# A two-layer image kernel (Fourier attention, then linear attention) on one core: its transfers merged into fewer and larger ones

## The chip, the core and the metric

The kernel runs on one core of one Trainium2 chip. Five engines work side by side: PE (TensorE, the matmuls), DVE (VectorE), ACT (ScalarE), POOL (GpSimd) and SP (SyncE, which here only issues transfers). Transfers are carried out by 16 DMA engines, which the core's issuing engines share; in this kernel nearly all are issued by SP, and those of the start by ACT as well. SBUF is the on-chip memory with 128 partitions, PSUM holds the matmuls' results, DRAM holds inputs, outputs and scratch.

The metric is the device time of one execution in microseconds. The kernel before has a median of 2763.84 us over three runs (2757.47 to 2765.46).

## What is computed

The input is a batch of 8 images of 256 channels and 96 x 96 pixels, f32. Cut to what matters, the reference is:

```python
def layer0(x, w1, b1, w2, b2, w3, b3, w_out, temperature):
    q, k, v = (fft2(conv1x1(x, w, b)) for w, b in ((w1, b1), (w2, b2), (w3, b3)))
    q, k, v = (t.reshape(b, 8, 32, 96 * 96) for t in (q, k, v))
    q, k = l2_normalize(q), l2_normalize(k)            # over the 9216 frequencies
    attn = einsum('bhcn,bhdn->bhcd', q, k) * temperature
    attn = complex(softmax(real(attn)), softmax(imag(attn)))
    out = abs(ifft2(einsum('bhcd,bhdn->bhcn', attn, v)))
    return conv1x1(out.reshape(b, 256, 96, 96), w_out)

def layer1(x, Wq, bq, Wk, bk, Wv, bv):                 # x as (b, 256, 9216)
    q, k = softplus(Wq x + bq), softplus(Wk x + bk)    # 32 channels each
    v = Wv x + bv
    return (q k-sum-normalised) @ (k v^T)              # linear attention

x = x + layer0(group_norm(x))
x = x + layer1(group_norm(x))
```

The group norm has 32 groups of 8 channels. The kernel doesn't take Fourier transforms of q, k and v. It gets the products of q and k out of sums over pixels, and replaces the transforms by a product of each image row with rows of its mirror image and by a fixed matrix R of 96 x 96 per row, which it calls rotating.

## The kernel before, in words

**Images and arenas.** The images are handled one after the other, image b+1's first part being woven into image b's last. Two large SBUF tiles (`arena`, 128 partitions x 2 halves x 9232 f32) take turns: image b's data is in `x_of(b)`, its rotated form in `y_of(b)`, which is the other arena. A half holds 128 of the 256 channels when the data is channel-major. In the first stage the arena's lower part (0 to `LO` = 4624) serves as staging space.

**Pair sums** (`pair_sums`, L342 to L415). The image's 96 rows are taken in pairs. A unit u (0 to 12) is four row pairs' worth on 128 partitions; two units are a double unit v = u // 2. `load_grouped` (L137) brings a double unit: f has the rows h and h+1 for four values of h, each on 32 partitions (4 DMAs of 192 KB), g has the mirror rows H-h and H-h-1, one at a time (8 DMAs of 96 KB). `turn_blocks(u)` (L355) copies the first element of every row of g behind its last (L361, once per double unit), transposes 32 x 32 blocks on DVE (L364, two instructions), and writes both turned blocks to a DRAM scratch `xtd` (L367, 2 DMAs of 384 KB). After an odd unit it issues the load of double unit v+2. The turned blocks have two places, by u % 2 (`turned_pair`). `pair(u)` forms their sum on POOL (L394) and their difference on DVE or POOL (L395; u = 0 and 12 on DVE alone, L390 to L392) into a tile `eo`, and sets its border columns (L385). `products` (L350) multiplies eo by itself on PE, 8 matmuls for each of three q; each q is a step of the generator. Around the products of unit u stand pair(u + 1), at q = 0, and turn_blocks(u + 2), at q = 1. The last unit (u = 12) is a single row.

**The tables** (`tables`, L249). Only once, beside image 0's pair sums: R's first form, computed on DVE, is written to DRAM (`rt`, L272), read back in 13 pieces in a skewed order (L279, `tm`), completed with two border columns and a tail by ACT (L290 to L292), and written out again as `rx` in 39 transfers (L295), one piece for each step of the generator. At the end comes `load_small` (L210): 55 small loads of biases and weights (L212 to L228), of which 32 are w_out's (`wo`). All are on ACT's queue. A POOL memset (L213) goes ahead of the biases `b12`.

**Rotating** (`rotate`, L595). `fetch` brings the turned rows from `xtd` back (L629, 192 KB: one direction c, two rows) and R's piece for four rows (L604) into one of 16 slots, which lie in the upper part of the image's arena; 14 steps ahead. `step` multiplies the rows by R on PE (L643) and copies the result into y (L649, L650). There are 49 steps an image, two for each even row h. From step 24 on, x itself is loaded again (`load_x`) in six pieces.

**The rest.** Layer 0's attention (`mix`), the image's complex parts (`images`, L666, with z on PE at L706, their magnitudes on DVE, POOL and ACT at L745 to L751, and w_out at L714), layer 1 (`layer1`, L765) and `output` (L939): there PE makes o (L974), DVE and POOL add it to x (L979, L983), and after both halves m of a piece s four DMAs (L995 to L997, 384 KB each) write the output, each with both halves.

**Order.** The order of the instructions on each engine is the order of the program text (a manual schedule); `weave` and the generators set what stands beside what. The main loop (L1011 on) runs image 0's pair sums with one step of `tables` at every index over 6, a `fetch` at every index over 20, and a `step` at every index over 26. In the later images the pair sums of b+1 are woven into `images(b)` and `layer1(b)`. Waits between engines and transfers are set by the framework from the memory that is touched; for an access that spans several rows of a tile it takes the whole stretch in between. [...]

## Time and profile before

| | |
|---|---|
| median of 3 runs | 2763.84 us (2757.47 to 2765.46) |
| profiled execution | 2761.41 us |
| its span | 2759.6 us |
| mean granted clock of TensorE | 0.959 |
| DMA packets | 388484, 413.37 MB, mean 150 GB/s |
| of these under 512 B | 144405 |
| SP's queue (q1) | 378880 packets, 406.20 MB, 53.5% of 16 engines |
| ACT's queue (q10) | 9400 packets, 4.49 MB, 0.7% |

The page's second section cuts the span into 40 equal slices of 69 us; a digit is the busy share in tenths. Its row for the DMA engines, and what they moved in GB/s:

```profile
DMA  7682736837185562746539274582736738177003
GB/s 173 189 259 50 182 81 199 246 58 186 53 272 172 120 164 73 237 147 148 136 106 290 72 177 107 163 259 56 184 79 222 223 69 197 36 240 221 1 7 138
```

The page's fifth section lists groups of instructions: line, engine, operation, out<-in, count, then busy time, mean ns of one, and idle time of the engine before them with what ended most of it. The page's sixth lists DMA issues by size. The groups that the change touches:

```profile
L350 PE MATMUL acc<-eo 128*128 128x257 f32 (+2 forms) x2368 | 439.7, 338 | 80.4 <-POOL eo L385 58.7
L394 POOL TENSOR_TENSOR eo<-arena 128x768 f32<-128x768 f32 x88 | 188.0, 2137 | 570.1 <-DVE ksum L901 254.4
L364 DVE STREAM_TRANSPOSE arena<-arena 128x768 f32<-128x768 f32 x192 | 175.8, 950 | 11.9 <-DMA xtd<-arena 8.9
```

In a list of waits, a line gives the waiting engine and line, what ended the wait, and then us in total, times, and the longest. A line of windows gives the stretch, its length, then busy us (and instructions) of PE, PE's weight loads, DVE, ACT and POOL, PE's granted clock, the DMA share and GB/s.

### The profile page before, as it was taken

To read this page: it belongs to the slowest core of one execution; us is meant where nothing else is said; L and a number is where in the kernel's file an instruction comes from. 1 tells how busy PE (TensorE), PEld (TensorE's weight loads), DVE (VectorE), ACT (ScalarE), POOL (GpSimd) and SP (SyncE) were. 2 spreads that over 40 slices of the span, in tenths; PEclk is the share of its full clock that TensorE was granted. 3 is DMA by queue.
4 is the path that set the end of the run, shared out by engine and by line. 5 is a ranking of instruction groups with operands and counts; after the bars stand their busy time and mean duration, and the time that the engine had idled before them with its cause. 6 is when DMAs were issued, how large, how long until landed. Compare 5 with 4: busy or idle time off the path is not lost. (4 is left out here: it accounts for less than half of the span.)

```text
span 2759.6 us, 41965 instructions
## 1 busy us (share of the span) xinstructions
PE 2553.8 (93%) x15580; PEld 1767.7 (64%) x15580; DVE 1804.9 (65%) x3441; ACT 1152.0 (42%) x1997; POOL 857.6 (31%) x801
## 2 busy tenths in 40 slices
PE   4499999999989999999999999999998999999987
PEld 3385666757667566766667566675666757667545
DVE  3257766577666767568675686657767577755766
ACT  0025353353534435344343544425353353524553
POOL 2203523135141451324412343213523135131311
PEclk8699999999999999899999999899999999989997
DMA  7682736837185562746539274582736738177003
GB/s 173 189 259 50 182 81 199 246 58 186 53 272 172 120 164 73 237 147 148 136 106 290 72 177 107 163 259 56 184 79 222 223 69 197 36 240 221 1 7 138
DMA packets 388484, 413.37 MB, mean 150 GB/s; under 512 B 144405, under 2 KB 339129, under 8 KB 388281
## 3 DMA queue, kind: packets, MB, share of 16 engines
q1 hardware_dynamic: 378880, 406.20, 53.5%
q10 hardware_dynamic: 9400, 4.49, 0.7%
q8 instruction: 124, 2.03, 0.3%
q14 instruction: 80, 0.65, 0.1%
HBM read 256.72 MB, written 153.86 MB: 149 GB/s over the span
## 5 line engine op out<-in xcount | busy, mean ns | idle before, releaser
L706 PE MATMUL z<-arena,mz 128*128 128x384 f32 (+1 forms) x2304 | 591.9, 488 | 0.0
L714 PE MATMUL po<-e,wo 128*128 128x384 f32 x1536 | 527.6, 487 | 1.7 <-ACT e L751 1.7
L750 POOL TENSOR_TENSOR e<-e 128x768 f32<-128x768 f32 x192 | 348.5, 1815 | 555.2 <-ACT e L749 528.5
L350 PE MATMUL acc<-eo 128*128 128x257 f32 (+2 forms) x2368 | 439.7, 338 | 80.4 <-POOL eo L385 58.7
L350 PEld LDWEIGHTS acc<-eo 128*128 128x128 f32 (+1 forms) x2368 | 386.5, 196 | 172.1 <-POOL eo L385 59.3
L706 PEld LDWEIGHTS z<-arena,mz 128*128 128x128 f32 (+1 forms) x2304 | 310.2, 163 | 234.6 <-issue 50.5
L643 PE MATMUL y<-tm,arena 96*128 96x128 f32 x3072 | 407.3, 289 | 31.5 <-ACT ys L650 12.6
L643 PEld LDWEIGHTS y<-tm,arena 96*128 96x128 f32 x3072 | 382.9, 201 | 77.3 <-issue 26.3
L714 PEld LDWEIGHTS po<-e,wo 128*128 128x128 f32 x1536 | 290.0, 190 | 204.7 <-ACT e L751 7.3
L745 DVE TENSOR_TENSOR e<-z,xT 128x768 f32<-128x768 f32 x384 | 361.8, 950 | 85.2 <-PE z L706 85.0
L749 ACT ACTIVATE e<-e 128x1536 f32<-128x1536 f32 x192 | 284.5, 1482 | 195.6 <-DVE e L745 194.0
L394 POOL TENSOR_TENSOR eo<-arena 128x768 f32<-128x768 f32 x88 | 188.0, 2137 | 570.1 <-DVE ksum L901 254.4
L716 DVE TENSOR_TENSOR arena<-arena,po 128x384 f32<-128x384 f32 x384 | 209.8, 552 | 192.9 <-PE po L714 192.9
L751 ACT ACTIVATE e<-e 128x768 f32<-128x768 f32 x192 | 162.0, 844 | 366.0 <-POOL e L750 362.1
L983 POOL TENSOR_TENSOR arena<-arena,po 128x384 f32<-128x384 f32 x180 | 179.3, 1015 | 292.5 <-ACT po L982 292.3
L306 DVE BATCH_NORM_STATS2 st<-arena 128x6 f32<-128x384 f32 x384 | 194.3, 548 | 0.0
L364 DVE STREAM_TRANSPOSE arena<-arena 128x768 f32<-128x768 f32 x192 | 175.8, 950 | 11.9 <-DMA xtd<-arena 8.9
L650 ACT COPY ys<-y 128x4 f32<-128x4 f32 (+1 forms) x200 | 32.6, 163 | 348.3 <-DVE arena L649 304.1
L875 PE MATMUL xT<-ident,arena 128*128 128x128 f32 x1152 | 157.9, 291 | 3.0 <-ACT xT L878 3.0
L982 ACT COPY po<-o 128x384 f32<-128x384 f32 x180 | 78.4, 485 | 183.5 <-PE o L974 178.9
L875 PEld LDWEIGHTS xT<-ident,arena 128*128 128x128 f32 x1152 | 138.7, 150 | 23.2 <-issue 13.6
L649 DVE COPY arena<-y 128x384 f32<-128x384 f32 (+1 forms) x200 | 108.8, 544 | 67.6 <-PE y L643 52.9
(225 smaller groups left out, 2512.8 us busy)
## 6 DMA issues: line engine op xcount, KB each, us to landing
xtd<-arena SPq DMA_DIRECT2D x192, 384.0 KB
arena<-xtd SPq DMA_DIRECT2D x384, 192.0 KB
arena<-in_x_dram SPq DMA_DIRECT2D x96, 768.0 KB
out_dram<-arena SPq DMA_DIRECT2D x192, 384.0 KB
arena<-in_x_dram SPq DMA_DIRECT2D x192, 192.0 KB
arena<-in_x_dram SPq DMA_DIRECT2D x384, 96.0 KB
tm<-rx SPq DMA_DIRECT2D x96, 159.0 KB
wl<-in_w1t_dram SPq DMA_DIRECT2D x8, 256.0 KB
```

The costliest lines, as they stand in the source:

```text
L306: nc.vector.bn_stats(out=st[:, k, c, :], in_=x_of(b)[:, k, c * CH:(c + 1) * CH])
L350: nc.tensor.matmul(acc[c][:, m * (C + 1):m * (C + 1) + C + 1 - m * P], lhsT=eo[0:np_, q, c, 1 + m * P:1 + (m + 1) * P], rhs=eo[0:np_, q, c ...
L394: nc.gpsimd.tensor_add(e, ft, gt)
L643: nc.tensor.matmul(pu[:, o:o + P], lhsT=xt[:, s, k * P:(k + 1) * P], rhs=tm[:, n:n + P], start=True, stop=True)
L706: nc.tensor.matmul(out[:, 0:CH].rearrange("p (h q) -> p h q", q=PR), lhsT=columns(mz, k, c, j), rhs=yz[:, k, f, :, o:o + PR], start=(k == ...
L714: nc.tensor.matmul(po[:, 0:CH], lhsT=wo[:, k, m * P:(m + 1) * P], rhs=e[:, k, :], start=(k == 0), stop=(k == KC - 1))
L716: nc.vector.tensor_add(x[:, m, n], x[:, m, n], po[:, 0:CH])
L745: nc.vector.tensor_add(e[:, 2 * c:2 * c + 2, :].rearrange("p t (q h) -> p t q h", h=H), pz[:, 0:CH].rearrange("p (h q) -> p q h", h=H).uns ...
L749: nc.scalar.activation(e, e, AF.Square)
L750: nc.gpsimd.tensor_add(e[:, 0:2, :], e[:, 0:2, :], e[:, 2:4, :])
L875: nc.tensor.transpose(pt[:, j * C + k * P:j * C + (k + 1) * P], x[:, k, o:o + P], ident)
L983: nc.gpsimd.tensor_add(x[:, m, r], x[:, m, r], t)
```

## The change

R is read back in one piece and written out in four transfers; it is completed by three ACT instructions in place of 39, in a part of the second arena that is free at the start. The table helpers on DVE move behind R. `load_small` has 28 transfers instead of 55 (w_out's first half, the temperatures and the layer-1 biases in one transfer each or nearly so) and yields between batches, so it goes on from step to step; `tables` is started before the loop and goes on from index 4 instead of 7. The mirror rows of g are loaded in pairs, in their order in memory (4 DMAs instead of 8; at h = 0 they stay single), and the transpose reads them backwards. The copy behind the rows' ends becomes two copies through a small tile `wrap`. The turned blocks of a double unit lie together, in one place per direction; one DMA of 1.5 MB, issued after the odd unit, writes them all, where four of 384 KB were. A `fetch` brings both directions of a row pair (384 KB), into 7 slots; it is called half as often. `output` issues the write of a half m right after its adds, two DMAs for each m.

```diff
     def turned(b):
-        o = NB8 * 2 * (2 * W + 1)
-        return [x_of(b)[:, u % 2, o + i * NQ * C:o + (i + 1) * NQ * C] for i in range(2)]
+        return [x_of(b)[:, c, TO:TO + 2 * NQ * C].rearrange("p (q r n) -> p q r n", q=NQ, r=2) for c in range(2)]
...
-            nc.sync.dma_start(out=f[s].rearrange("p c r w -> p c (r w)"), in_=xs[:, :, h:h + 2].rearrange("p c r w -> p c (r w)"))
-            for r in range(2):
-                nc.sync.dma_start(out=g[s, :, r, 0:W], in_=xs[:, :, (H - h - r) % H])
+            nc.sync.dma_start(out=f[s], in_=xs[:, :, h:h + 2].rearrange("p c r w -> p c (r w)"))
+            if h:
+                nc.sync.dma_start(out=g[s], in_=xs[:, :, H - h - 1:H - h + 1].rearrange("p c r w -> p c (r w)"))
+            else:
+                nc.sync.dma_start(out=g[s, :, 0:W], in_=xs[:, :, H - 1])
+                nc.sync.dma_start(out=g[s, :, W:2 * W], in_=xs[:, :, 0])
...
     def load_small():
-        for c, v in enumerate((wkt, wqt)):
-            nc.scalar.dma_start(out=wkq0[:, :, c, :], in_=v.rearrange("(k p) o -> p k o", p=P))
         nc.gpsimd.memset(b12[0:64], 0.0)
+        yield
         for c, v in enumerate((b1, b2)):
             for m in range(KC):
                 nc.scalar.dma_start(out=b12[32 * m:32 * m + 1, c, :], in_=v[m * P:(m + 1) * P].unsqueeze(0))
...
+        nc.scalar.dma_start(out=wo[:, 0, :], in_=bass.AP(wot.tensor, wot.offset, [[C, 16], [HEAD * C, NH], [1, C]]))
         for j in range(16):
-            for k in range(KC):
-                c = (j, HEAD - j if j else 16)[k]
-                nc.scalar.dma_start(out=wo[NH * j:NH * j + NH, k, :], in_=wo_v[c])
+            nc.scalar.dma_start(out=wo[NH * j:NH * j + NH, 1, :], in_=wo_v[HEAD - j if j else 16])
+            if j % 4 == 3:
+                yield
...
-        for i in range(4):
-            load(i)
-        for i in range(NP + 1):
-            yield
...
-            for q in range(NQ):
-                dst = rx[i].rearrange("(j q) w -> q j w", q=NQ)[q] if i < NP else rx[i][32 * q:32 * q + 32]
-                nc.scalar.dma_start(out=dst[:, 0:o], in_=flat[32 * q:32 * q + 32, 0:o])
-            if i + 4 <= NP:
-                load(i + 4)
+        big = y_of(0)[0:W, 1, 0:(N + 1) * (W + 2) + P - W]
+        rows = big[:, 0:(N + 1) * (W + 2)].rearrange("p (r w) -> p r w", r=N + 1)
+        v = rt[0:N + 1, 1:]
+        nc.scalar.dma_start(out=rows[:, :, 1:W + 1], in_=bass.AP(v.tensor, v.offset, [[1, W], [2 * W, N + 1], [1, W]]))
...
+        yield
+        for q in range(NQ):
+            s = slice(32 * q, 32 * q + 32)
+            v = big[s, 0:NP * TR * (W + 2)]
+            src = bass.AP(v.tensor, v.offset, [list(v.ap[0]), [TR * (W + 2), NP], [1, RW]])
+            nc.scalar.dma_start(out=rx[0:NP].rearrange("i (j q) w -> q j i w", q=NQ)[q], in_=src)
+        nc.scalar.dma_start(out=rx[NP][:, 0:P + 2], in_=big[:, N * (W + 2):N * (W + 2) + P + 2])
+        yield
...
         def turn_blocks(u):
...
-                nc.vector.tensor_copy(g[:, :, :, W], g[:, :, :, 0])
+                nc.vector.tensor_copy(wrap, g[:, 0:SG:W])
+                nc.vector.tensor_copy(g[:, W:SG + 1:W], wrap)
...
-                for c, t in enumerate((ft, gt)):
-                    nc.sync.dma_start(out=xtd[c, u], in_=t)
...
-            if r and v + 2 <= NG // 2:
-                load_grouped(b, v + 2)
+            if r:
+                nc.sync.dma_start(out=xtd[:, v].rearrange("c p m -> p c m"), in_=x_of(b)[:, :, TO:TO + 2 * NQ * C])
+                if v + 2 <= NG // 2:
+                    load_grouped(b, v + 2)
...
         def fetch():
...
-                a, u = h // 2 % G, h // (2 * G) * 2
-                nc.sync.dma_start(out=xts[i], in_=xtd[c, u:u + 2, 32 * a:32 * a + 32].rearrange("u j (q n) -> (j q) u n", q=NQ))
+                v, a = divmod(i, G)
+                nc.sync.dma_start(out=xts[i], in_=xtd[:, v, 32 * a:32 * a + 32].rearrange("c j (q m) -> (j q) c m", q=NQ))
...
         if fetch:
-            for _ in range(13):
+            for _ in range(6):
                 fetch()
...
+                for j in range(2):
+                    o = columns_of(s, j) // CH
+                    out_c, x_c = (v.rearrange("p (f n w) -> p f n w", f=2, w=CH)[:, :, o] for v in (out_v[b, :, m], x[:, m, 0:HW]))
+                    nc.sync.dma_start(out=out_c, in_=x_c)
...
-            for j in range(NB):
-                r = slice(columns_of(s, j), columns_of(s, j) + CH)
-                nc.sync.dma_start(out=out_v[b, :, :, r], in_=x[:, :, r])
...
         parts = tables()
+        next(parts)
         fetch, turns = rotate(0)
         for i, _ in enumerate(sums):
-            if i > 6:
+            if i > 3:
                 next(parts, None)
-            if i > 20:
+            if i > 20 and i % 2 == 0:
                 fetch()
```

More of the change, by code (lines that the diff above doesn't have):

```diff
@@ L123, in load_x, with staged, turned @@
         nc.sync.dma_start(out=x_of(b)[:, :, t * TW:(t + 1) * TW], in_=x_v[b, :, :, t * TW:(t + 1) * TW])
-    def staged(b, v):
-        r = x_of(b)[:, v % 2, 0:LO]
-        o = NB8 * 2 * W
-        return (r[:, 0:o].rearrange("p (c r w) -> p c r w", c=NB8, r=2),
-                r[:, o:o + NB8 * 2 * (W + 1)].rearrange("p (c r w) -> p c r w", c=NB8, r=2))
-    def turned_pair(b, u):
-        o = NB8 * 2 * (2 * W + 1)
-        return [x_of(b)[:, u % 2, o + i * NQ * C:o + (i + 1) * NQ * C] for i in range(2)]
+    SG = NB8 * 2 * W
+    TO = 2 * SG + 4
+    def staged(b, v, at=0):
+        return x_of(b)[:, v % 2, at * SG:at * SG + SG + at]
+    def turned(b):
+        return [x_of(b)[:, c, TO:TO + 2 * NQ * C].rearrange("p (q r n) -> p q r n", q=NQ, r=2) for c in range(2)]
     def load_grouped(b, v):
-        f, g = staged(b, v)
         xs = x[b].rearrange("(c i) h w -> i c h w", i=32)
@@ L142, in load_grouped @@
             m = H // 2
-            f = f.rearrange("p c r w -> p (c r w)")[:, 0:C].rearrange("p (c w) -> p c w", c=NB8)
-            g = g.rearrange("p c r w -> p (c r w)")[:, 0:C].rearrange("p (c w) -> p c w", c=NB8)
+            f, g = (staged(b, v, i)[:, 0:C].rearrange("p (c w) -> p c w", c=NB8) for i in range(2))
             for q in range(NQ):
@@ L151, in load_grouped @@
             return
+        f, g = (staged(b, v, i)[:, 0:SG].rearrange("p (c w) -> p c w", c=NB8) for i in range(2))
         for a in range(G):
             h, s = 2 * (G * v + a), slice(32 * a, 32 * a + 32)
-            nc.sync.dma_start(out=f[s].rearrange("p c r w -> p c (r w)"), in_=xs[:, :, h:h + 2].rearrange("p c r w -> p c (r w)"))
-            for r in range(2):
-                nc.sync.dma_start(out=g[s, :, r, 0:W], in_=xs[:, :, (H - h - r) % H])
+            nc.sync.dma_start(out=f[s], in_=xs[:, :, h:h + 2].rearrange("p c r w -> p c (r w)"))
[4 more added lines that the diff above has]
+                nc.sync.dma_start(out=g[s, :, W:2 * W], in_=xs[:, :, 0])
     setup = y_of(0)[:, 0, :]
@@ L216, in load_small @@
                 nc.scalar.dma_start(out=b12[32 * m:32 * m + 1, c, :], in_=v[m * P:(m + 1) * P].unsqueeze(0))
-        nc.scalar.dma_start(out=b3col, in_=b3.rearrange("(k p) -> p k", p=P))
-        temp_f = temp.rearrange("h a b -> h (a b)")
-        for h in range(C // HEAD):
-            k, j = divmod(h, 4)
-            nc.scalar.dma_start(out=tcol[32 * j:32 * j + 32, k:k + 1], in_=temp_f[h].partition_broadcast(HEAD))
-        for j in range(4):
-            nc.scalar.dma_start(out=bkq4[32 * j:32 * j + 32, 0:1], in_=bk.unsqueeze(1))
-            nc.scalar.dma_start(out=bkq4[32 * j:32 * j + 32, 1:2], in_=bq.unsqueeze(1))
+        yield
+        for c, v in enumerate((bk, bq)):
+            nc.scalar.dma_start(out=bkq4[:, c:c + 1], in_=bass.AP(v.tensor, v.offset, [[0, 4], [1, 32], [1, 1]]))
+        for k in range(KC):
+            nc.scalar.dma_start(out=tcol[:, k:k + 1], in_=bass.AP(temp.tensor, temp.offset + 4 * k, [[1, 4], [0, HEAD], [1, 1]]))
+        yield
+        for c, v in enumerate((wkt, wqt)):
+            nc.scalar.dma_start(out=wkq0[:, :, c, :], in_=v.rearrange("(k p) o -> p k o", p=P))
+        nc.scalar.dma_start(out=b3col, in_=b3.rearrange("(k p) -> p k", p=P))
+        yield
+        nc.scalar.dma_start(out=wo[:, 0, :], in_=bass.AP(wot.tensor, wot.offset, [[C, 16], [HEAD * C, NH], [1, C]]))
         for j in range(16):
-            for k in range(KC):
-                c = (j, HEAD - j if j else 16)[k]
-                nc.scalar.dma_start(out=wo[NH * j:NH * j + NH, k, :], in_=wo_v[c])
+            nc.scalar.dma_start(out=wo[NH * j:NH * j + NH, 1, :], in_=wo_v[HEAD - j if j else 16])
+            if j % 4 == 3:
+                yield
     csn = const.tile([P, 3, H], F32, name="csn")
@@ L244, in two_layer_kernel @@
     rx = dram.tile([NP + 1, W, RW], F32, name="rx")
-    xtd = dram.tile([2, NG, P, NQ * C], F32, name="xtd")
+    xtd = dram.tile([2, NG // 2, P, 2 * NQ * C], F32, name="xtd")
     xtm = dram.tile([W, C], F32, name="xtm")
     def tables():
-        nc.vector.reduce_sum(rep4[:, 0:D], ident.rearrange("p (j d) -> p d j", d=D), axis=AX.X)
-        for j in range(1, 4):
-            nc.vector.tensor_copy(rep4[:, 32 * j:32 * j + 32], rep4[:, 0:D])
-        nc.vector.tensor_copy(sel8.rearrange("p (i d) -> p i d", d=D), rep4[:, 0:8].unsqueeze(2).to_broadcast([P, 8, D]))
-        for j in range(4):
-            o = HEAD * j
-            nc.vector.tensor_copy(gsel[:, 0:16, j], gri[:, o:o + 16])
-            nc.vector.tensor_copy(gsel[:, 17:32, j], gri[:, P + o + 1:P + o + 16])
-            nc.vector.tensor_copy(gsel[:, 32, j:j + 1], gri[:, o + 16:o + 17])
         pcs = ps_tile("pcs")
@@ L272, in tables @@
         nc.scalar.dma_start(out=rt, in_=t0[:, 3 * W:5 * W])
-        flats = {}
-        def load(i):
-            flats[i] = tm_tile(f"tm0_{i}")
-            n = TR if i < NP else 1
-            v = rt[TR * i:TR * i + n, 1:]
-            nc.scalar.dma_start(out=flats[i][:, 0:n * (W + 2)].rearrange("p (r w) -> p r w", r=n)[:, :, 1:W + 1],
-                                in_=bass.AP(v.tensor, v.offset, [[1, W], [2 * W, n], [1, W]]))
-        for i in range(4):
-            load(i)
-        for i in range(NP + 1):
-            yield
-            flat = flats.pop(i)
-            n = TR if i < NP else 1
-            tm = flat[:, 0:n * (W + 2)].rearrange("p (r w) -> p r w", r=n)
-            o = n * (W + 2) + P - W
-            nc.scalar.copy(tm[:, :, 0:1], csn[0:W, 2, TR * i:TR * i + n].unsqueeze(2))
-            nc.scalar.mul(tm[:, :, W + 1:W + 2], csn[0:W, 2, TR * i:TR * i + n].unsqueeze(2), -1.0)
-            nc.scalar.copy(flat[:, n * (W + 2):o], csn[0:W, 2, 0:P - W])
-            for q in range(NQ):
-                dst = rx[i].rearrange("(j q) w -> q j w", q=NQ)[q] if i < NP else rx[i][32 * q:32 * q + 32]
-                nc.scalar.dma_start(out=dst[:, 0:o], in_=flat[32 * q:32 * q + 32, 0:o])
-            if i + 4 <= NP:
-                load(i + 4)
@@ new lines, in tables @@
+        big = y_of(0)[0:W, 1, 0:(N + 1) * (W + 2) + P - W]
+        rows = big[:, 0:(N + 1) * (W + 2)].rearrange("p (r w) -> p r w", r=N + 1)
+        v = rt[0:N + 1, 1:]
+        nc.scalar.dma_start(out=rows[:, :, 1:W + 1], in_=bass.AP(v.tensor, v.offset, [[1, W], [2 * W, N + 1], [1, W]]))
+        nc.scalar.copy(rows[:, :, 0:1], csn[0:W, 2, 0:N + 1].unsqueeze(2))
+        nc.scalar.mul(rows[:, :, W + 1:W + 2], csn[0:W, 2, 0:N + 1].unsqueeze(2), -1.0)
+        nc.scalar.copy(big[:, (N + 1) * (W + 2):], csn[0:W, 2, 0:P - W])
@@ new lines, in tables @@
+        yield
+        for q in range(NQ):
[4 more added lines that the diff above has]
+        nc.scalar.dma_start(out=rx[NP][:, 0:P + 2], in_=big[:, N * (W + 2):N * (W + 2) + P + 2])
+        yield
+        for j in range(4):
+            o = HEAD * j
+            nc.vector.tensor_copy(gsel[:, 0:16, j], gri[:, o:o + 16])
+            nc.vector.tensor_copy(gsel[:, 17:32, j], gri[:, P + o + 1:P + o + 16])
+            nc.vector.tensor_copy(gsel[:, 32, j:j + 1], gri[:, o + 16:o + 17])
@@ L298, in tables @@
+        nc.vector.reduce_sum(rep4[:, 0:D], ident.rearrange("p (j d) -> p d j", d=D), axis=AX.X)
+        for j in range(1, 4):
+            nc.vector.tensor_copy(rep4[:, 32 * j:32 * j + 32], rep4[:, 0:D])
+        nc.vector.tensor_copy(sel8.rearrange("p (i d) -> p i d", d=D), rep4[:, 0:8].unsqueeze(2).to_broadcast([P, 8, D]))
         nc.vector.tensor_scalar_mul(csn[:, 0:2, N + 1:H], csn[:, 0:2, N + 1:H], -1.0)
-        load_small()
+        yield from load_small()
     def tm_tile(name):
@@ L353, in products @@
                                      skip_group_check=True)
+        wrap = two.tile([P, 2 * NB8], F32, tag="wrap", name=f"wrap_{b}")
         def turn_blocks(u):
             v, r = divmod(u, 2)
-            f, g = staged(b, v)
-            ft, gt = turned_pair(b, u)
-            if u < NG and r == 0:
-                nc.vector.tensor_copy(g[:, :, :, W], g[:, :, :, 0])
-            if u < NG:
-                for t, src in ((ft, f[:, :, r, :]), (gt, g[:, :, r, W:0:-1])):
-                    nc.vector.transpose(out=t.rearrange("p (q c i) -> p q c i", q=NQ, c=NB8),
-                                        in_=src.rearrange("p c (q w) -> p q c w", q=NQ))
-                for c, t in enumerate((ft, gt)):
-                    nc.sync.dma_start(out=xtd[c, u], in_=t)
-            else:
-                f = f.rearrange("p c r w -> p (c r w)")[0:W, 0:C].rearrange("p (c w) -> p c w", c=NB8)
-                g = g.rearrange("p c r w -> p (c r w)")[0:W, 0:C].rearrange("p (c w) -> p c w", c=NB8)
-                nc.vector.tensor_copy(g[0:32, :, 31:32], f[0:32, :, 0:1])
-                nc.vector.transpose(out=ft[0:W, 0:C].rearrange("p (c i) -> p c i", c=NB8), in_=f)
-                nc.vector.transpose(out=gt[0:W, 0:C].rearrange("p (c i) -> p c i", c=NB8), in_=g[:, :, ::-1])
-                nc.sync.dma_start(out=xtm, in_=ft[0:W, 0:C])
@@ L375, in turn_blocks @@
-            if r and v + 2 <= NG // 2:
-                load_grouped(b, v + 2)
+            t = turned(b)
+            if u == NG:
+                f, g = (staged(b, v, i)[0:W, 0:C].rearrange("p (c w) -> p c w", c=NB8) for i in range(2))
+                nc.vector.tensor_copy(g[0:32, :, 31:32], f[0:32, :, 0:1])
+                for i, src in enumerate((f, g[:, :, ::-1])):
+                    nc.vector.transpose(out=t[i][0:W, 0, 0].rearrange("p (c i) -> p c i", c=NB8), in_=src)
+                nc.sync.dma_start(out=xtm, in_=t[0][0:W, 0, 0])
+                return
@@ new lines, in turn_blocks @@
+            f = staged(b, v, 0).rearrange("p (c r w) -> p c r w", c=NB8, r=2)
+            if r == 0:
+                g = staged(b, v, 1)
+                nc.vector.tensor_copy(wrap, g[:, 0:SG:W])
+                nc.vector.tensor_copy(g[:, W:SG + 1:W], wrap)
+            o = SG + (1 - r) * W + 1
+            g = x_of(b)[:, v % 2, o:o + SG].rearrange("p (c n) -> p c n", c=NB8)[:, :, W - 1::-1]
+            for i, src in enumerate((f[:, :, r], g)):
+                nc.vector.transpose(out=t[i][:, :, r].rearrange("p q (c i) -> p q c i", c=NB8),
+                                    in_=src.rearrange("p c (q w) -> p q c w", q=NQ))
@@ L378, in pair @@
+            if r:
+                nc.sync.dma_start(out=xtd[:, v].rearrange("c p m -> p c m"), in_=x_of(b)[:, :, TO:TO + 2 * NQ * C])
+                if v + 2 <= NG // 2:
+                    load_grouped(b, v + 2)
         def pair(u):
-            ft, gt = turned_pair(b, u)
             eo = ring_tile(f"eo_{b}_{u}").rearrange("p (q c n) -> p q c n", q=NQ, c=2)
             nq, np_ = (NQ, P) if u < NG else (1, W)
-            ft, gt = (t[0:np_, 0:nq * C].rearrange("p (q n) -> p q n", q=nq) for t in (ft, gt))
+            ft, gt = (t[0:np_, 0:nq, u % 2] for t in turned(b))
@@ L608, in rotate @@
         area = x_of(b)
-        slots = [area[0:W, k, o + 2 * C * i:o + 2 * C * (i + 1)].rearrange("p (r n) -> p r n", r=2)
-                 for k, o, n in ((0, LO, 7), (1, LO, 6), (0, LO + 14 * C, 2), (1, LO + NS * CH + 4 * CH, 1)) for i in range(n)]
-        assert LO + 9 * 2 * C <= AW and LO + 6 * 2 * C <= LO + NS * CH + 2 * CH
+        slots = [area[0:W, k, o + 4 * C * i:o + 4 * C * (i + 1)].rearrange("p (c m) -> p c m", c=2)
+                 for k, o, n in ((0, LO, 3), (1, LO, 3), (0, LO + 12 * C, 1)) for i in range(n)]
+        assert LO + 16 * C <= AW and LO + 12 * C <= LO + NS * CH + 2 * CH
         xts, tms = {}, {}
@@ L618, in fetch @@
             at_[0] += 1
-            if i >= len(order):
+            if i > G * NG // 2:
                 return
-            c, h, piece = order[i]
-            if piece not in tms:
-                tms[piece] = load_r(piece)
+            h = 2 * i
+            if h // TR not in tms:
+                tms[h // TR] = load_r(h // TR)
             xts[i] = slots[i % len(slots)]
             if h == N:
-                nc.sync.dma_start(out=xts[i][:, 0], in_=xtm)
+                nc.sync.dma_start(out=xts[i][:, 0, 0:C], in_=xtm)
             else:
-                a, u = h // 2 % G, h // (2 * G) * 2
-                nc.sync.dma_start(out=xts[i], in_=xtd[c, u:u + 2, 32 * a:32 * a + 32].rearrange("u j (q n) -> (j q) u n", q=NQ))
+                v, a = divmod(i, G)
+                nc.sync.dma_start(out=xts[i], in_=xtd[:, v, 32 * a:32 * a + 32].rearrange("c j (q m) -> (j q) c m", q=NQ))
         def step(i):
             c, h, piece = order[i]
-            tm, xt = tms[piece], xts.pop(i)
+            tm, xt = tms[piece], xts[i // 2][:, c].rearrange("p (r n) -> p r n", r=2)
             rows = [0] if (c, h) in ((1, 0), (0, N)) else [0, 1]
@@ L654, in steps @@
             for i in range(len(order)):
-                while at_[0] < min(i + len(slots) - 2, len(order)):
+                while at_[0] < min(i // 2 + len(slots) - 1, len(order) // 2 + 1):
                     fetch()
```

## The prediction

> **What bounds the kernel now.** I read the page's busy shares and 40 slices first, then PE's waits, its timeline and the windows of the start, then SP's waits, the steady image and the tail.

> ```profile
> PE 2553.8 (93%) x15580; PEld 1767.7 (64%) x15580; DVE 1804.9 (65%) x3441; ACT 1152.0 (42%) x1997; POOL 857.6 (31%) x801
> ...
> PE   4499999999989999999999999999998999999987
> ```

> PE is the bound in all but two slices (69 us each): the first two hold 4 tenths, the last two a little less than full. The change touches only transfers (and a few DVE copies that serve them), so it can pay only where PE waits for them. PE's waits from 0 to 160 us:

> ```profile
> PE acc L350 <- POOL eo L385: 58.7, 3, 20.8
> PE acc L350 <- DVE eo L391: 16.9, 1, 16.9
> PE y L643 <- DMA arena<-xtd: 4.0, 1, 4.0
> ```

> That is 79.6 us, and behind 160 us no wait of PE in the list is on a DMA (the longest, kT on DVE, is 28.1 us in 16 waits). L385 is the pair sum, whose input is turned by DVE (L364) out of a loaded double unit of eight row pairs. PE's timeline (start, duration, group):

> ```profile
> 54.37 10.98 PE L350 MATMUL acc<-eo 128*128 128x257 f32 x48 [18.03 <-POOL eo L385]
> 85.26 10.91 PE L350 MATMUL acc<-eo 128*128 128x257 f32 x48 [19.90 <-POOL eo L385]
> 116.93 6.50 PE L350 MATMUL acc<-eo 128*128 128x257 f32 x24 [20.77 <-POOL eo L385]
> 127.46 1.13 PE L643 MATMUL y<-tm,arena 96*128 96x128 f32 x8 [4.03 <-DMA arena<-xtd]
> ```

> One double unit about every 31 us, 11 us of work in it; from 127.46 PE runs through. Are the DMA engines full meanwhile? Windows (PE, PEld, DVE, ACT, POOL busy, clock, DMA share, GB/s):

> ```profile
> 0.00:20.00 20.00, 3.10 (x9) 2.71 (x10) 7.99 (x31) 1.57 (x2) 3.38 (x62) 1.00 1.08 179
> 60.00:80.00 20.00, 5.36 (x32) 4.65 (x31) 0.34 (x2) 2.14 (x15) 0.00 (x0) 0.76 0.56 147
> 80.00:100.00 20.00, 10.91 (x48) 9.48 (x48) 5.68 (x6) 1.22 (x9) 5.52 (x5) 0.73 0.46 125
> ```

> Full (1.08) only at first; then half idle. So the start is bound by the order of transfers. SP's waits there:

> ```profile
> SPq L156 <- DMA rx<-tm: 15.4, 6, 4.3
> SPq L156 <- DMA tm<-rt: 9.6, 1, 9.6
> ...
> SPq L367 <- DMA rx<-tm: 6.8, 2, 5.9
> SPq L154 <- DMA rx<-tm: 6.1, 2, 4.7
> ```

> Loads of x (L154, L156) and block writes (L367) wait for ACT's R transfers, with which they share no buffer. In the built program each transfer of SP and ACT takes one of eight completion counters in turn, and so waits for the transfer eight places earlier in their common order. The R pieces (13 loads, 39 writes) and 55 small loads are strewn into this order, and drag the loads of x down to their own pace.

> **The start, part by part.** I follow the changed program's order of transfers with durations from rows.

> - *R in one piece*: R is written to DRAM (rt) as soon as `tables()` runs, at about 6 us (32.09 before), and read back at once: its landing takes 2.2 us (before, rt issued 32.09, its reader 34.27). The single load (1.8 MB) starts at 8.2 beside double units 0 and 1. 13 loads and 39 writes become 1 and 4.
> - *Loads of x*: 1.57 MB a double unit. At 179 to 190 GB/s that is 8.5 us. Here two measures of the mirror pairs differ. The row: 179 GB/s at a full share, whereas the output at the end, 128 partitions a transfer, has 388 at 1.06. [...]By packets alone (768 B where 384 B were, the mirror half of the bytes) one might hope for the rate of the tail, 4 us a double unit, 4 units on the path: 18 us. [...]
> - *Block write of a double unit*: 1.57 MB at the tail's 388 GB/s is 4.0 us, and 2.2 to land: 6.2 us. It adds waits: the access spans both halves of the arena, so a write of an even double unit waits for the loads of the next odd one, an odd load for the write before it, and the first transpose of the next double unit for the write of the last (one turned buffer where two were). Behind the waiting SP entry stand the next loads; behind the waiting transpose stand the sums on DVE, then POOL, then PE.
> - *Small loads*: 55 become 28. Before, 55 took from 86.4 to 111.1 us, the 32 of w_out 0.36 us each. [...]the row says 0.36 to 0.45 because many are in flight, so 27 x 0.4 = 11 us. I take the row.

> Chain: units 0 and 1 (3.1 MB) and R's 1.8 MB share the engines: done at 27 (at 190 GB/s for 4.9 MB 26 us, plus the start). Write 0 is issued at 27, lands at 34; transposes and sum of unit 2 are done at 39. Behind that sum, on POOL, stands the memset of b12, the first thing that the small loads need: they run from 40, woven into unit 2's load, 28 x 0.45: done at 52.5. Then serially: write 1 to 57, load 3 to 67, write 2 to 73.5, load 4 to 81, write 3 to 86, load 5 to 95.5, fetch 0, write 4 from 97.5 to 104. The transposes of u = 10 then stand at 104 (125.2 before). The second rotated fetch reads what write 4 may touch, so it lands at 106.5; PE has by then done the first two steps and two of u = 9's products. Before, the third step began at 133.16; now at 106.5. **Gain 26 us**. Bounds: 38 if R does not slow unit 1 and small loads vanish beside x; 12 if R starves unit 1 (+6), small loads go at 0.7 us (+7) or write latencies are 1 us longer each.

> **Steady images** (seven). PE's wait list has no DMA there, so smaller numbers of transfers gain nothing. The costs: one small DVE copy more per double unit (L361, 48 now: 0.17 us at the least, 0.49 in the median), 1 to 3 us of DVE an image, hidden in the 35% in which DVE idles; 7 to 20 us in all if it were not. The transpose at an even u now waits for a write issued after the odd one before it: in the image at 615 to 705 us the odd transposes end at 627.2, 642.9, 664.6 and 682.8, the next even begin at 633.2, 654.0, 670.9 and 687.9: gaps 6.0, 11.1, 6.3, 5.1 against 6.2 plus whatever the queue holds ahead (up to 1 us): short by 0 to 1.8. DVE has cover there:

> ```profile
> 674.47 0.96 DVE L745 TENSOR_TENSOR e<-z,xT 128x768 f32<-128x768 f32 x1 [1.73 <-PE z L706]
> ...
> 692.61 0.56 DVE L716 TENSOR_TENSOR arena<-arena,po 128x384 f32<-128x384 f32 x1 [2.86 <-PE po L714]
> ```

> idle 1.73 and 2.86 behind the third and fourth of these; behind the first (633) none. So 0 to 1 us an image: +3 in all; without cover, 2 an image, +14. The rotated fetches become half as many with seven double slots where sixteen single were: their lead falls from 14 steps to about 12, of 2.2 us or more each, hidden. The loads behind the longer write are late by 2 us, beside five PSUM buffers of products.

> **The tail.** Windows of the output's end:

> ```profile
> 2736.00:2740.00 4.00, 4.00 (x20) 3.92 (x18) 3.60 (x9) 0.96 (x2) 2.25 (x3) 0.50 1.05 382
> 2752.00:2756.00 4.00, 0.00 (x0) 0.00 (x0) 0.00 (x0) 0.00 (x0) 0.11 (x1) 0.66 1.06 388
> ```

> The 9.4 MB of the last image leave at the full rate, ending after PE does. Writing each half as soon as its adds are done starts this stream 0.9 us sooner: -1.

> **Sum**, against the profiled execution (span 2759.6, 1.8 around it, 2761.4, which is 2.4 below the median 2763.84 and inside the three runs): 2761.4 - 26 - 1 + 3 = **2737**.

> **Rivals.**
> - *The serial waits don't bite* (0.15): units and writes overlap, and the start is near what the bytes need: 9.4 MB of x at 200 GB/s (47 us), 7.9 MB of writes (20), R both ways (9), first tables and latencies (14): PE runs through from about 90, a gain of 41 to 43: 2720. For it: the DMA share of a half. Against: the waits are in the program.
> - *The gain is eaten* (0.13): R beside unit 1, small loads in front of unit 2 and writes that delay each next load give back 15 to 22: a gain of 4 to 11, 2752 to 2758. For it: 179 GB/s is already the limit in the first 20 us, and R is 1.8 MB more there.
> - *Slower* (0.06): the single turned buffer. If a write of 1.57 MB lands not 6 but 10 us after its issue, since rotated loads, x and output share the engines, each of two or three even transposes per image stalls DVE by 4 us, half of it uncovered: 5.5 an image, 7 images: 38 against 27, 2773. It decides from 4 us of PE an image on. For it: in the slices the steady images move up to 290 GB/s; against: the queue is short where the transposes lie.
> - *It does not do what it says*: x stays at 8.5 us a unit with pairs; that is inside my sum.

> **Numbers.** My forecast's chance is 0.66, its own range 2724 to 2750. To hold 8 in 10 I reach into the first rival and the second: 2718 to 2753. Runs of this kernel spread by 8 us, so 0.3% (8.3 us) is about what can be told from no change. Faster by more: 0.66 and 0.15 and a third of the second rival, 0.86; within: 0.08; slower: 0.06.

> **What will show it.** PE's waits on L385 and L391 before 130 us fall from 76 to about 50; its first L643 comes near 100 to 107 us instead of 127.46; ACT's small loads lie at 40 to 53. In steady images a DVE wait L364 on DMA xtd of 0 to 2 us at even u, and no DMA in PE's waits. The end's output starts 1 us sooner after the last image's first adds. Wrong it is if PE's waits behind 160 us grow by over 10 us, or if the first L643 is later than 118 or before 92.

## The result, and the profile after

The changed kernel takes 2744.15 us (median of 5 runs, 2738.91 to 2750.13), the kernel before 2765.0 us (5 runs, 2757.47 to 2765.84). The ratio is 0.993, with a 95% interval of 0.991 to 0.995: 20.85 us less. The profiled execution of the changed kernel took 2738.91 us, its span is 2737.1 us, 22.5 less than before.

The page of the changed kernel: busy shares, two rows of slices, and two of the groups that were shown of before (L343 was L350, L369 was L364).

```profile
PE 2553.0 (93%) x15580; PEld 1768.7 (65%) x15580; DVE 1817.2 (66%) x3489; ACT 1145.5 (42%) x1961; POOL 857.3 (31%) x801
...
PE   3799998999999998999989999999998999989988
...
DMA  8872718546184562836539264582626727186003
...
L343 PE MATMUL acc<-eo 128*128 128x257 f32 (+2 forms) x2368 | 436.9, 337 | 49.2 <-POOL eo L382 21.9
...
L369 DVE STREAM_TRANSPOSE arena<-arena 128x768 f32<-128x768 f32 x192 | 175.7, 953 | 32.0 <-DMA xtd<-arena 21.6
```

PE does the same work in the same busy time. What changed is the start: the second slice went from 4 to 7 (the first from 4 to 3), and the idle time before the pair products, 49.2 us instead of 80.4. DVE pays for a part of it: it now waits 21.6 us for block writes where it waited 8.9. PE's waits from 0 to 160 us (in total, times, longest):

```profile
PE acc L343 <- POOL eo L382: 21.9, 3, 15.4
PE acc L343 <- DVE eo L388: 12.1, 1, 12.1
PE acc L343 <- POOL eo L391: 10.0, 1, 10.0
PE y L640 <- DMA arena<-xtd: 9.9, 2, 6.9
```

The three waits for pair sums make 44.0 us where there were 75.6. In PE's timeline a double unit now comes every 17 to 26 us instead of 31:

```profile
36.95 10.47 PE L343 MATMUL acc<-eo 128*128 128x257 f32 x48 [10.03 <-POOL eo L391]
62.83 11.17 PE L343 MATMUL acc<-eo 128*128 128x257 f32 x48 [15.41 <-POOL eo L382]
79.40 9.74 PE L343 MATMUL acc<-eo 128*128 128x257 f32 x48 [5.40 <-POOL eo L382]
...
97.49 1.13 PE L640 MATMUL y<-tm,arena 96*128 96x128 f32 x8 [3.01 <-DMA arena<-xtd]
...
108.56 2.08 PE L640 MATMUL y<-tm,arena 96*128 96x128 f32 x8 [6.87 <-DMA arena<-xtd]
```

And SP's waits in the same stretch:

```profile
SPq L372 <- DMA arena<-in_x_dram: 17.1, 9, 7.3
SPq L372 <- DMA arena<-xtd: 15.0, 2, 8.5
SPq L152 <- DMA xtd<-arena: 10.9, 2, 5.7
...
SPq L152 <- DMA b<-in_b_dram: 8.2, 1, 8.2
```

R's pieces are gone from the list. In their place stand the waits that the change added: block writes (L372) for loads of x and for a rotated fetch, loads (L152) for block writes; and the small loads are still there (b).

A landmark splits the time. The first group-norm matmul of image 0's rotated form (gm_a) starts at 155.28 us before and at 133.11 after: of the 22.5 us between the two profiled executions, 22.2 are gained by then. The later part differs by 0.3 us only, but in pieces that go both ways, as shown below.

### The profile page after: what moved, and what is told of

It reads as the page before. It is cut to its first block, busy times and chain, and to the rows that moved or that the text cites. A ratio compares the mean times of both kernels' runs of the same rounds, so it can differ in the third digit from the quotient of the medians.

```text
span 2737.1 us, 41164 instructions
## 1 busy us (share of the span) xinstructions
PE 2553.0 (93%) x15580; PEld 1768.7 (65%) x15580; DVE 1817.2 (66%) x3489; ACT 1145.5 (42%) x1961; POOL 857.3 (31%) x801
## 5 line engine op out<-in xcount | busy, mean ns | idle before, releaser
L343 PE MATMUL acc<-eo 128*128 128x257 f32 (+2 forms) x2368 | 436.9, 337 | 49.2 <-POOL eo L382 21.9
L343 PEld LDWEIGHTS acc<-eo 128*128 128x128 f32 (+1 forms) x2368 | 384.4, 195 | 140.5 <-issue 47.7
L640 PE MATMUL y<-tm,arena 96*128 96x128 f32 x3072 | 406.8, 288 | 37.4 <-ACT ys L647 12.6
L391 POOL TENSOR_TENSOR eo<-arena 128x768 f32<-128x768 f32 x88 | 188.5, 2142 | 555.1 <-DVE ksum L898 255.9
L369 DVE STREAM_TRANSPOSE arena<-arena 128x768 f32<-128x768 f32 x192 | 175.7, 953 | 32.0 <-DMA xtd<-arena 21.6
```

The source lines that it names most:

```text
L343: nc.tensor.matmul(acc[c][:, m * (C + 1):m * (C + 1) + C + 1 - m * P], lhsT=eo[0:np_, q, c, 1 + m * P:1 + (m + 1) * P], rhs=eo[0:np_, q, c ...
L391: nc.gpsimd.tensor_add(e, ft, gt)
L640: nc.tensor.matmul(pu[:, o:o + P], lhsT=xt[:, s, k * P:(k + 1) * P], rhs=tm[:, n:n + P], start=True, stop=True)
```

## The experiments

Each run was measured beside the kernel before on the same chip. The table gives the median, the ratio with its 95% interval, and from the profile (one execution of each kernel) the start of gm_a in image 0.

| kernel | median us | before | ratio | gm_a at us |
|---|---|---|---|---|
| before | 2765.0 | | | 155.3 |
| changed | 2744.15 | 2765.0 | 0.993 (0.991 to 0.995) | 133.1 |
| r_pieces | 2766.72 | 2761.02 | 1.0021 (1.0013 to 1.0029) | 150.1 |
| tables_only | 2737.16 | 2761.02 | 0.9903 (0.9885 to 0.9921) | 134.6 |
| small55 | 2746.33 | 2761.02 | 0.9936 (0.9922 to 0.9951) | 138.5 |
| single_rows | 2755.2 | 2761.02 | 0.9973 (0.9961 to 0.9984) | 147.5 |
| single_from2 | 2745.69 | 2761.0 | 0.9936 (0.9914 to 0.9957) | 134.9 |
| unit_writes | 2740.36 | 2761.0 | 0.9925 (0.9909 to 0.9942) | 126.0 |
| unit_late_sp | 2727.26 | 2761.0 | 0.9877 (0.9863 to 0.9892) | 120.0 |
| r_later | 2727.55 | 2761.26 | 0.9875 (0.985 to 0.99) | 113.0 |
| wrap_act | 2704.8 | 2761.26 | 0.9792 (0.976 to 0.9825) | 120.0 |
| both_late | 2715.81 | 2760.38 | 0.9832 (0.9796 to 0.9868) | 112.6 |
| after_wrap_act | 2725.32 | 2760.38 | 0.9887 (0.9854 to 0.992) | 137.4 |
| before_wrap_act | 2734.94 | 2760.38 | 0.9915 (0.9894 to 0.9936) | 154.6 |

**R in pieces again** (r_pieces).

```diff
-        big = y_of(0)[0:W, 1, 0:(N + 1) * (W + 2) + P - W]
...
+        for i in range(4):
+            load(i)
+        for i in range(NP + 1):
+            yield
...
```

> The changed kernel with R read and written in 13 pieces again (13 loads, 39 writes), all else as changed. Theory: the pieces drag the loads of x as before; 10 to 20 us of the gain go. Rival (R's 1.8 MB in one piece beside unit 1 costs as much as the pieces did): within 5 us of the changed kernel, with block 0 written earlier than 25 us.

gm_a comes at 150.1 us, 17.0 later than in the changed kernel. The theory holds: SP's loads and block writes wait 47.9 us for R's reads and writes again, and without R in one piece the rest of the change gains 5.2 us by gm_a. The edit moves something else as well: the pieces take 13 steps of `tables`, so the small loads come at 84.6 to 97.1 us instead of 38.7 to 53.1. SP waits for them there (13.0 us) instead of at double unit 2, so the 17.0 us are the price of the pieces with this shift, not of the pieces by themselves. In time the kernel is even 0.2% slower than the one before: what it gains by gm_a it loses later.

**The tables alone** (tables_only): the kernel before with `tables`, `load_small` and their start from the changed one, and nothing else.

```diff
+        next(parts)
...
-            if i > 6:
+            if i > 3:
                 next(parts, None)
```

> The kernel before with only the tables of the changed one: R in one piece, 28 small loads, the earlier start of both; rows, block writes, fetches and output as before. Theory (the drag of ACT's transfers is nearly all of the gain, and the longer block write takes some back): 20 to 30 us below the kernel before, as much as the whole change or more. Rival (row pairs and large writes carry half of it): about 10 us below.

gm_a at 134.6: 20.7 us of the change's 22.2 by this part alone. The time is at least as good as that of the whole change. So row pairs, block writes, fetches and output together bring almost nothing net. The next runs show that this is a sum of gains and losses, though not all of its parts were measured singly.

**55 small loads again** (small55).

```diff
-        nc.scalar.dma_start(out=wo[:, 0, :], in_=bass.AP(wot.tensor, wot.offset, [[C, 16], [HEAD * C, NH], [1, C]]))
         for j in range(16):
-            nc.scalar.dma_start(out=wo[NH * j:NH * j + NH, 1, :], in_=wo_v[HEAD - j if j else 16])
+            for k in range(KC):
+                c = (j, HEAD - j if j else 16)[k]
+                nc.scalar.dma_start(out=wo[NH * j:NH * j + NH, k, :], in_=wo_v[c])
```

> The changed kernel with the 55 small loads of before, in the same batches and places. Theory: 27 more in front of unit 2's last quarters, at 0.4 us each 11 us: the write of block 1 is issued at about 63 us instead of 52.5, and the time stands 10 us below the kernel before instead of 21. Rival (they are hidden by other waits): still 21 below.

The second block write is issued at 53.6 us instead of 52.5, the third at 73.3 instead of 68.2; gm_a is 5.4 us later. Merging them is worth 5 us, half of what I had. ACT's queue issues small loads until 66.6 us instead of 53.1, so more than half of these 13.5 us run beside something else.

**Single mirror rows** (single_rows, then single_from2 with single rows only in loads 2 to 5 of image 0).

```diff
-            if h:
+            if h and (b or v < 2):
                 nc.sync.dma_start(out=g[s], in_=xs[:, :, H - h - 1:H - h + 1].rearrange("p c r w -> p c (r w)"))
```

> The changed kernel with its mirror rows loaded singly again (8 DMAs of 96 KB a double unit). Theory [...]: [...]the last product of image 0 ends at about 134 us instead of 129, the time stands about 16 us below the kernel before instead of 21. Rival (the gain comes from the packets under 512 B that went away): most of the gain goes, under 8 us remain.

> The changed kernel with single mirror rows in loads 2 to 5 of image 0 alone; its first two loads and all later images keep the pairs, so that unit 1's loads stand in the same places of the common order of transfers as in the changed kernel. Theory (pairing pays by places in that order: with single rows unit 1's third quarter waited 15.8 us for R's write[...]): block 0 written at 25 us as in the changed kernel, the last product of image 0 about 5 us later, at 132. Rival (it is the rate or the packets): 10 to 14 us later, as with all rows single.

With all rows single gm_a comes 14.4 us later, three times the 5 us expected. SP's waits of that kernel, 0 to 45 us, show where:

```profile
SPq L152 <- DMA rx<-arena: 15.8, 1, 15.8
```

The traces show the common order: from 160 us on the transfers of SP and ACT, 1502 in the kernel before and 1026 in the changed one, signal eight semaphores (the counters) strictly in turn, and of all 1759 in the kernel before 1149 are recorded as waiting for the semaphore that they signal themselves. With 24 loads of x instead of 17 in front, the third quarter of double unit 1 stands eight places behind R's first write. That write waits for the whole of R to be read. So one load of x is held for 15.8 us, and block 0 is written at 41.1 us instead of 25.1. Where only the later loads are single, double unit 1 stands where it stood, block 0 goes at 24.5, and gm_a comes 1.8 us later. So the pairs of the four later loads pay 1.8 us, and those of the first two 12.6. These 12.6 are put down to the places in the common order, since the one wait of 15.8 us is longer than that; what the rate of the first two loads adds was not measured by itself. It is the same drag as R's pieces. The same wait (14.4 us) is in the tables-only kernel, whose rows are single too.

**A write for each unit** (unit_writes): both turned blocks of a unit side by side in one half of the arena, one DMA of 768 KB, two buffers.

```diff
-    def turned(b):
+    def turned(b, u):
...
-            if r:
-                nc.sync.dma_start(out=xtd[:, v].rearrange("c p m -> p c m"), in_=x_of(b)[:, :, TO:TO + 2 * NQ * C])
-                if v + 2 <= NG // 2:
-                    load_grouped(b, v + 2)
+            nc.sync.dma_start(out=xtd[u], in_=x_of(b)[:, u % 2, TO:TO + 2 * NQ * C])
+            if r and v + 2 <= NG // 2:
+                load_grouped(b, v + 2)
```

> The changed kernel with a block write for each unit (768 KB, one DMA, both directions side by side in one half of the arena), so that two turned buffers are in use again and no write spans both halves; fetches move the same bytes in the same packets. Theory (the span and the single buffer cost what the tables gained beyond 22 us): no block write waits for loads of x, the transposes at even u do not wait for a write; the last product of image 0 ends 10 to 15 us sooner, at 112 to 117, and the steady images lose 0.5 us each: about 37 us below the kernel before. Rival (the loads' rate bounds the start anyway): within 3 us of the changed kernel.

gm_a comes at 126.0, 7.1 us sooner; less than the 10 to 15 expected. The span and the single buffer, with the larger transfer (the three were not told apart), cost 7 us of the start. The rest of the expected gain met the next wait; SP's waits of this kernel, 0 to 60 us, have a new first line:

```profile
SPq L372 <- DMA rx<-arena: 16.3, 1, 16.3
```

The second unit's write now stands eight places behind R's first write. Its transposes end at 19 us and it is issued at about 35, and unit 2's loads are behind it on SP. In time, the interval of unit_writes overlaps that of the changed kernel; the gain of 7 us is shown by the landmark alone.

**Small loads late, from SP** (unit_late_sp), **and R late as well** (r_later).

```diff
-        nc.scalar.dma_start(out=b3col, in_=b3.rearrange("(k p) -> p k", p=P))
+        nc.sync.dma_start(out=b3col, in_=b3.rearrange("(k p) -> p k", p=P))
...
-            if i > 3:
+            if 3 < i < 6 or i > 24:
                 next(parts, None)
```

> As the writes by unit, and the 28 small loads issued from SP's queue from index 25 of the first image's sums on, behind nearly all its loads of x. Theory (small loads stand in front of unit 2's quarters from 38 to 53 us): unit 2's load lands near 37 instead of 52, the last product of image 0 ends at 95 to 103, about 50 us below the kernel before. Rival (some other transfer, or PE's own products, is late next): no more than 5 us better than the writes by unit.

> As the kernel with writes by unit and late small loads, but R is read back behind unit 2's loads and written behind unit 4's, both from SP's queue; small loads from index 27 on. Theory (R's 1.8 MB beside unit 1, and its writes, which hold the second block write from 18 to 35 us, delay the first units): unit 1 is turned at 19 us instead of 26, block writes follow at once, the last product of image 0 ends 5 to 9 us sooner, at 107 to 111; 55 us or more below the kernel before. Rival (the engines' total work bounds the start: the same bytes go later): within 3 us.

gm_a goes to 120.0 with the small loads late, and to 113.0 with R read behind unit 2's loads and written behind unit 4's. The first step is 6 us at gm_a and 13 us in the time (2727.26 against 2740.36; 7.6 us between the two profiled executions). It is 34 us below the kernel before where I expected 50: the second block write still waits for R until 35 us. The second moves gm_a by 7.0 us, where 5 to 9 were expected, but the time does not move (2727.55 against 2727.26). A part of what the start gains is given back in image 0 itself: from its gm_a to the next it is 311.0 us instead of 306.8, with 2.7 us more of PE's busy time. That led to the last runs.

**The steady images.** The prediction put 3 us of loss on the single turned buffer. DVE's waits of the changed kernel from 160 us on:

```profile
DVE arena L369 <- DMA xtd<-arena: 2.0, 7, 0.4
```

0.4 us at most, once an image. Yet PE's idle time did rise. Windows from one gm_a to the next, images 3 to 4 and 4 to 5 (length, then busy us of PE, PEld, DVE, ACT, POOL, then clock, DMA share, GB/s). Before:

```profile
1123.90:1456.80 332.90, 318.82 (x1951) 220.01 (x1947) 223.86 (x421) 143.43 (x246) 108.67 (x95) 0.97 0.56 153
1456.80:1786.00 329.20, 314.52 (x1951) 217.11 (x1947) 225.33 (x423) 143.82 (x247) 109.10 (x96) 0.98 0.57 156
```

The changed kernel:

```profile
1111.50:1442.00 330.50, 316.07 (x1952) 218.68 (x1948) 225.87 (x427) 143.13 (x245) 108.61 (x95) 0.98 0.54 153
1442.00:1768.90 326.90, 311.72 (x1952) 215.63 (x1948) 225.66 (x428) 143.37 (x246) 109.14 (x96) 0.99 0.54 156
```

Length less busy is PE's idle time: 14.1 and 14.7 us before, 14.4 and 15.2 after; over all seven stretches 99.6 and 102.6, the 3 us forecast. But with a write for each unit, and so without the single buffer, the seven stretches still hold 101.5, and DVE doesn't wait for a block write there. So at most 1.1 us is the buffer's. (tables_only, whose steady code is that of before, holds 97.5: sums of this kind scatter by 2 us.)

Most of the 3 us is one wait. PE's longest in an image is kT, for DVE; image 4 before, in the changed kernel and in wrap_act, which follows below:

```profile
1715.72 0.90 PE L864 MATMUL kT<-ident,arena 128*128 128x128 f32 x3 [3.02 <-DVE arena L844]
1701.36 0.90 PE L861 MATMUL kT<-ident,arena 128*128 128x128 f32 x3 [3.37 <-DVE arena L841]
1681.04 0.88 PE L861 MATMUL kT<-ident,arena 128*128 128x128 f32 x3 [4.55 <-DVE arena L841]
```

It is 3.02 to 3.03 us in all seven images before and 3.36 to 3.38 after, 2.4 us in all. On DVE, which works without a pause there, two copies through wrap (0.17 and 0.18 us) stand in front of the transposes, the pair difference and the L841 that kT waits for; before, it was one copy of 0.17 us.

The reader should see a second thing: the stretches differ by up to 9 us in PE's *busy* time, for the same matmuls, with the granted clock (0.96 to 0.99). That is three times the loss in question.

**The wrap copies on ACT** (wrap_act on the kernel with late small loads; after_wrap_act on the changed one; before_wrap_act on the one before, which has one copy).

```diff
-                nc.vector.tensor_copy(wrap, g[:, 0:SG:W])
-                nc.vector.tensor_copy(g[:, W:SG + 1:W], wrap)
+                nc.scalar.copy(wrap, g[:, 0:SG:W])
+                nc.scalar.copy(g[:, W:SG + 1:W], wrap)
```

> As the kernel with writes by unit and late small loads, but with the two copies through wrap on ACT instead of DVE. The steady images keep 15.2 us of PE idle time each where the kernel before has 14.1 to 14.7, also without the single turned buffer. Theory (the second copy and its place on DVE cost it): idle time falls by 0.4 us or more an image, 3 us in all, and DVE's busy time by 2 us an image. Rival (it comes from the later loads behind the longer write, or the fetches' new order): idle time stays at 15.2 and the time within 2 us of the kernel with late small loads.

> The changed kernel with nothing but its two wrap copies on ACT. Theory (these copies on DVE shift the steady images so that PE's granted clock falls for 10 to 20 us in some of them): images of 328 us each with a mean granted clock of 0.99, 20 us below the changed kernel. Rival (with the single turned buffer other timings rule): images of 330 to 336 us stay, within 3 us of the changed kernel.

> The kernel before with its one copy behind the rows (L361) on ACT instead of DVE. Theory (it is the copy's place on DVE that costs, in both kernels): images of 328 us, 15 to 20 us below the kernel before. Rival (only the second copy, or the new layout, brought it): within 5 us of the kernel before.

Both expectations for wrap_act fell: PE's idle time did not go down but up, and the time fell by 22 us against the kernel with late small loads. The idle time rose at kT (4.53 to 4.55 us an image): DVE's transposes now wait for ACT's copies, 10.2 us an image. The same two stretches of wrap_act:

```profile
1092.20:1420.00 327.80, 311.25 (x1952) 215.01 (x1948) 220.91 (x416) 145.76 (x259) 109.22 (x96) 0.99 0.56 156
1420.00:1747.70 327.70, 311.12 (x1951) 214.94 (x1947) 220.88 (x416) 145.71 (x259) 109.12 (x96) 0.99 0.54 156
```

16.6 us idle, but 311.1 to 311.3 busy at a clock of 0.99, and five of the seven stretches are like this. The other two kernels repeat it: images of 327.6 to 328.1 us with the changed kernel's start (gm_a at 137.4) and with the old one's (154.6). So moving the copies from DVE to ACT brings 14 to 25 us in each of the three kernels (the differences of their distances to the kernel before), in PE's busy time and with a higher granted clock, and it has nothing to do with the merged transfers. In the changed kernel it delays the start by 4.3 us: block 0 is written at 32.3 us.

**All together** (both_late).

> Both of the last two: writes by unit, small loads late, R later from SP's queue, and the copies through wrap on ACT. Theory (the start and the granted clock of the steady images are separate): the last product of image 0 at 107 to 111 us as with R later, and 327.7 us an image as with the copies on ACT: about 63 us below the kernel before. Rival (the clock pattern depends on the exact timing of the first images): within 5 us of the kernel with the copies on ACT alone, either way.

The start is as expected (gm_a at 112.6), but the time is 44.6 us below the kernel before, not 63: in the profiled execution three of the seven stretches are 332 to 336 us long again, at a clock of 0.96 to 0.98. Its runs lie between 2698.6 and 2717.9 us. Its median is 11 us above that of wrap_act, outside the rival's 5, but by their intervals the two can't be told apart; wrap_act has the best median, 2704.8 us, 2.1% below the kernel before (ratio 0.9792, 0.976 to 0.9825).

## Why the prediction was right, and where it was not

Forecast: 2737 us for an execution like the profiled one, range 2718 to 2753. Measured: 2744.15 in the median, 2738.91 in the profiled execution. The profiled one is the fastest of the five runs, so that it lies only 2 us from the forecast is partly luck; the median is 7 us off, inside the range. Point by point:

- **The bound.** Right. PE gained only in the start, where it waited for transfers held by other transfers. r_pieces shows that R's pieces, with the small loads that they push back, were most of that drag: 17 of 22 us.
- **The chain of the start.** Right nearly everywhere. Forecast and trace: block 0 written at 27 and 25.1 us, unit 2 down and block 1 written at 52.5 and 52.5, load 3 from 57 and 58.1, write 2 at 67 and 68.2, write 4 at 97.5 and 97.55, the transposes of u = 10 at 104 and 105.1. PE's first rotating step came at 97.49 (named: 100 to 107), and its waits for pair sums fell to 44.0 us (about 50).
- **The gain of 26 us.** The third step came at 108.56, not 106.5: 24.6 us gained there. By gm_a 22.2 are left, since PE, having waited 6.87 us just before, runs slowly at first: this step takes 2.08 us where later ones take 1.06, the next product 2.78 where later ones take 1.48. The clock after a wait was not in my sum. Of the 3.8 us by which this term was too large, 2.4 are that (the granted clock is 0.50 from 106.6 to 113.4 us); the rest is the later third step.
- **Row pairs.** A step that failed. I expected 5 us of the pairs (134 instead of 129), an estimate that no trace showed; the hope by packets alone was 18. The chain takes 7.5 to 10 us for each of the loads 3 to 5, not the 4 of the tail's rate. Measured alone, the four later loads gain 1.8 us, nowhere near 18; but all the pairs are worth 14.4, because they move double unit 1's loads out of the place eight behind R's write in the common order. I had that order in hand and used it for R and the small loads alone.
- **Small loads.** 11 us forecast, 5.4 measured.
- **Added waits.** I let them run through the chain but gave them no price of their own; the write by unit shows 7 us.
- **Steady images.** +3 us forecast, 3.1 us of PE's idle time measured, for the wrong reason: at most 1.1 is the single buffer's, inside a scatter of 2. The second copy through wrap, which I hid in the time in which DVE idles, stands on DVE's way to kT, where DVE does not idle; it costs 0.35 us an image, 2.4 in all.
- **The tail.** -1 forecast. From the last image's first layer-1 matmul to the end it is 99.1 us before and 98.0 after; tables_only, with the old writes, has 99.3. The output runs at 392 GB/s while PE is busy and at 345 behind it:

```profile
2724.00:2728.00 4.00, 4.00 (x21) 2.98 (x16) 3.08 (x8) 0.96 (x2) 1.61 (x3) 0.50 1.06 392
2732.00:2736.00 4.00, 0.00 (x0) 0.00 (x0) 0.00 (x0) 0.03 (x1) 0.99 (x1) 0.50 0.91 345
```

- **The rivals.** The start near the limit of the bytes did not come with this change, but it exists: r_later reaches 42 us of gain at gm_a, what I had worked out for it, when SP waits for neither R's reads and writes nor small loads any more. The slower case did not come; the price on which it hung, a block write landing 4 us late for an even transpose in each image, is 0.4 us at most.

## What to carry to other kernels

Before counting what a merged transfer saves in bytes and packets, list which transfers share completion counters and in which order: here a load that needed nothing was held for 15.8 us by a slow transfer eight places ahead of it (single_rows), and the order was worth 17 us for R's pieces (the small loads' shift included) and 12.6 us for the row pairs. A merged transfer also merges its waits: in the changed kernel the writes over both halves of the arena waited 17.1 us for loads of x in the first 160 us, in nine waits. An engine that idles a third of the time can still stand on the path at one place: here a second copy of 0.17 to 0.18 us did, at 0.35 us an image. Where two kernels differ by under 1%, compare PE's busy time and granted clock over equal stretches before explaining the rest.

## What had not been expected of the hardware

PE's clock is worth as much here as the change: the copies on ACT bring 14 to 25 us, the change 20.85. At one place half the clock stands beside a long wait: in the changed kernel PE waited 6.87 us and then, at a granted clock of 0.50, ran a step in 2.08 instead of 1.06 us. But it isn't idle time alone. wrap_act has 16.6 us of it an image and a clock of 0.99; before has 14.1 to 14.7 in its six full images and 0.97 to 0.98. In the changed kernel's seven stretches PE has half the clock for 98.9 us, of which 71.7 lie within 27 us of a gm_a, around the output stage, where no wait of PE is longer than 1.62 us.

At the end of the changed kernel PE has half the clock from 2697.3 us on, though from 2710 to 2730 us it is busy all the time:

```profile
2700.00:2710.00 10.00, 8.70 (x38) 4.26 (x32) 5.20 (x7) 0.48 (x1) 1.00 (x1) 0.50 0.00 1
2710.00:2720.00 10.00, 10.00 (x47) 9.49 (x45) 8.79 (x20) 2.40 (x5) 4.45 (x5) 0.50 0.91 338
2720.00:2730.00 10.00, 10.00 (x46) 8.05 (x42) 8.22 (x18) 2.19 (x5) 4.52 (x5) 0.50 1.06 392
```

Ten of ten us busy, at 0.50, for 20 us on end: here a busy PE does not have the full clock. The matmuls there are o (L971), with 32 rows. Their shape alone is not the reason: in the kernel before, the same matmuls have the full clock from 2743.1 us on. What it is stays open. Runs of one kernel lie up to 19 us apart (both_late, 2698.6 to 2717.9); that its images meet the grid at other places from run to run would explain it, but only one execution of each kernel was profiled.
